# Layer 3's block mix as diagonal matmuls on TensorE, with the gathers of layers 2 and 3 cut and reordered by quarters

## The chip, the cores and the metric

The program runs on one core of a Trainium2 chip. A core has TensorE (PE: matmuls; its weight loads are shown as PEld), VectorE (DVE), ScalarE (ACT), GpSimd (POOL) and SyncE (SP), each with its own instruction queue, which they execute in order; they wait for each other by semaphores. Transfers go through 16 DMA engines. The metric is the device time of one execution in microseconds (us); lower is better.

## The reference

Input: x of 4 sequences of 1,024 tokens of width 128, float32. Four layers, each an attention-like block and a feed-forward block, with a residual and a layer norm after each:

```
x = layernorm(x + L2_attn(x))     # 16 causal heads of width 8
x = layernorm(x + L2_ffn(x))      # 8 experts, the best 2 of each token
x = layernorm(x + L3_attn(x))
x = layernorm(x + L3_ffn(x))      # 32 experts, the best 4, and a shared expert
```

(the last two of the four layers). The change is about L3_attn, and about the rows that the experts of L2_ffn and L3_ffn hand back. L3_attn takes the first axis, the 4 sequences, as the one that it mixes over; every position stands for itself:

```
rms = |q| / sqrt(128);  x = q / (rms + 1e-8)
u = silu(x @ u_w + u_b);  v = silu(x @ v_w + v_b)      # 256 features each
y[i] = sum over j of coefficient(head, i - j) * v[j]    # i, j = 0..3: the sequences
out = (u * y) @ o_w + o_b + q
```

The sum over j is a Toeplitz product over the 4 sequences: seven coefficients, for the lags -3 to 3, for each of 8 heads of 32 features. So in a layout with features on the partitions, a coefficient is a number for each partition.

## The kernel before, in words

x stays in SBUF as 32 tiles of 128 tokens x 128. Eight tiles are a quarter (the same 256 positions of all 4 sequences). Layer 3's parts are a (quarters 0 and 1, "the first half"), b (the third quarter) and c (the fourth). Layer 2's experts have parts too: a2 is the first half, m2 sequences 0 and 1 of the second half, n2 sequences 2 and 3 of it.

**Experts.** A route computes for each token the experts, the weights and the positions in a list ordered by expert (`posl2n`, `posl3a` and so on are these positions; DVE does nearly all of it, with `positions`, L1231). `spread` (L1307) writes the rows of x to the list in HBM by indirect DMAs of POOL, one for each tile and choice (`l3ra<-x`). The experts read the list in order, 512 rows at a time (`gathered`, L1322, `xg<-l3ra`): PE transposes (`tp`), multiplies by gate and up weights (`gu`), ACT takes silu (`sg`), DVE the product (`hg`), PE transposes it and multiplies by the down weights (`yp`), and the rows go back to HBM (`l3ya<-yg`). `collect` (L1350) gathers a token's rows by indirect DMAs of POOL into a tile `yt` and adds them to x with their weights on DVE (L1361). With 8 tiles of `yt`, the ninth gather waits for the adds of the first tile. Layer 3's parts have 64 (a), 32 (b) and 32 (c) indirect DMAs each way; m2 and n2 have 16 each way.

**Attention of layer 3** (`l3_attn`, L1512). For each quarter: norm (L185: statistics L191 and L192, the root, then one DVE `tensor_scalar` for each of 8 tiles, L205), the rms of each token by a square (L1548), a sum (L1549) and a root, the scaled copy `sq`, and x replaced by 2x + o_b (L1564). PE transposes `sq`, multiplies by the weights of v and u; silu on ACT (L1531), for part a by a tanh on ACT and two DVE operations (L1535, L1536), since other exponentials run beside it (`exps`). Then, for each of two groups of 128 features, four output sequences i and four input sequences j, a DVE operation on 128x256: the first a product (L1590), the others multiply-adds (L1592), and a product with u (L1594 or L1596). PE multiplies by o_w (`py`), DVE adds it to x (L1605), and a second norm and transposes follow.

**Order.** A planner written as Python generators writes out each engine's order. `mix` (L233) takes a step of a main generator and then as many steps of a side generator as its declared costs (the numbers that are yielded) fill; `chain` puts generators one after the other, `abreast` interleaves by declared cost, `press` (L1800) runs the side alone until something is done. In each queue the side's instructions keep the place that they got. The stretch that matters, from L1824 `all`:

- main `l2_attn(1)`, the second half's attention of layer 2; side: part a's rows of layer 2 gathered and added, `l3_attn(a)`, `l3_route(a)` and its scatter, with the routes of m2 and n2 in between;
- main `l2_experts(m2)`, with the same side, then `press` until n2's list is written and the route of a done;
- main `l2_experts(n2)`; side: the scatter of a, the gathers of m2 (`rows_in`);
- main shared expert and experts of layer 3 for a; side: the gathers of n2, attention and route of b, then the scatter of b and the gathers of all of a (`last(a)`: `collect`, `finish`), abreast with attention and route of c, then the scatter of c and the gathers of b;
- main shared expert and experts for b, then for c, with the same side; and at the end `close(c)`, the gathers of c with the last norm.

Of the kernel before, what the change touches and what calls it, by code (L numbers as in the profile page):

```python
# [14 lines left out]
AF = mybir.ActivationFunctionType  # L15
# [5 lines left out]
P = 128  # L21
# [48 lines left out]
def tile_of(b, i):  # L70

    return i // 2 * QT + b * 2 + i % 2


class Kernel:
# [109 lines left out]
    def norm(self, tiles, by="act"):  # L185
# [11 lines left out]
        else:  # L197
            ve = self.tile(self.small, [P, n], f"ve{n}")
            nc.vector.tensor_scalar(ve, mv[:, :, 1], LN_EPS, None, ALU.add)
            if by == "pool":  # L200
                nc.gpsimd.tensor_tensor(rstd, ve, self.mhalf[:, :n], ALU.pow)
            else:
                self.rsqrt(rstd, ve)
        for t, x in enumerate(tiles):
            nc.vector.tensor_scalar(x, x, mv[:, t, 0:1], rstd[:, t : t + 1], ALU.subtract, ALU.mult)  # L205
# [1144 lines left out]
    def collect(self, lay, part, k, yp, first=0, nt=None):  # L1350
# [15 lines left out]
        for t in range(first, first + (nt or part.nt)):  # L1366
# [145 lines left out]
    def l3_attn(self, part, exps=False):  # L1512
# [5 lines left out]
        with ExitStack() as ctx:  # L1518
# [19 lines left out]
            for q in range(part.q0, part.q0 + part.nq):  # L1538
                s = slice(q * QT, (q + 1) * QT)
                self.norm(self.quarter(q), by="dve" if exps else "act")  # L1540
                yield (7.0,)
                xq = self.tile(vp, [P, QC], "xq")
                rms = self.tile(self.small, [P, QT], "rms")
                for g in range(2):
                    sg = slice(q * QT + g * 4, q * QT + g * 4 + 4)
                    r = rms[:, g * 4 : g * 4 + 4]
                    sq = self.tile(vp, [P, 4, D], "sq")
                    nc.vector.tensor_tensor(sq, x[:, sg, :], x[:, sg, :], ALU.mult)  # L1548
                    nc.vector.tensor_reduce(r, sq, AX.X, ALU.add)  # L1549
# [524 lines left out]
```

## Time and profile before

| what | value |
|---|---|
| time, median of 15 runs | 2529.88 us (2516.64 to 2544.39) |
| the profiled execution's own time | 2531.99 us |
| its span in the profile | 2530.1 us, granted clock 0.825 |
| busy: PE, DVE, ACT, POOL | 67%, 53%, 33%, 30% |
| layer 2's second attention | 1262 to 1680 us |
| experts of m2, then n2 | 1680 to 1795, 1795 to about 1950 |
| shared expert and experts of layer 3, part a | 1951 to 2114 |
| the same for b, for c | to about 2350, to 2476 |
| the gathers of c and the end | 2476 to 2530 |

The profile names an instruction by its line in the kernel, its engine and operation, and the tiles that it writes and reads (`y<-v,ld,y`). A helper's line stands for all that the helper does: L157 is every matmul, L165 every transpose, L1295 every indirect DMA. "Idle before" is the time that the engine stood before such an instruction, and what released it. In the chain of waits, "issue" and "another core or an unknown queue" are times for which the profile shows no work that was waited for; on one core, the second can only be a handoff whose sender had been done earlier.

### The profile page before, as it was taken

How to read it: one execution, taken by the hardware profiler on the slowest of the kernel's cores; microseconds unless marked ns; L12 is line 12 of the kernel's file. 1: busy time of each engine (PE TensorE's matmuls, PEld its weight loads, DVE VectorE, ACT ScalarE, POOL GpSimd, SP SyncE). 2: the span in 40 equal slices, each digit the busy share in tenths (PEclk: the TensorE clock that was granted, in tenths of full speed). 3: DMA queues.
4: the chain of work that ended last, by engine and by line, in shares of the span. 5: the costliest groups of instructions: out<-in, count | busy, mean ns of one | idle time of the engine just before them, and what ended most of it. 6: DMA issues, size and time to landing. Idle time of an engine off the chain costs nothing.

```text
span 2530.1 us, 28678 instructions
## 1 busy us (share of the span) xinstructions
PE 1704.3 (67%) x9605; PEld 1033.4 (41%) x9605; DVE 1344.9 (53%) x3801; ACT 829.2 (33%) x1193; POOL 769.8 (30%) x701
## 2 busy tenths in 40 slices
PE   7535775985652864877878788978718896373490
PEld 3224333852320433755523232345415684162280
DVE  8857894655550643334536674654603575263363
ACT  5510461432320431322246454622202353131140
POOL 5521384136045004213231002001470204536404
PEclk9756788997775977998889898988869998587795
DMA  9900002434100032312210000030410231132242
GB/s 306 288 2 0 16 34 87 120 129 160 47 30 38 27 125 91 106 47 59 84 54 16 1 1 18 1 128 32 167 64 23 81 115 65 39 108 76 67 126 60
DMA packets 225736, 192.05 MB, mean 76 GB/s; under 512 B 17009, under 2 KB 204273, under 8 KB 225073
## 3 DMA queue, kind: packets, MB, share of 16 engines
q1 hardware_dynamic: 204880, 147.28, 18.4%
q0 software_dynamic: 20704, 42.86, 5.4%
q8 instruction: 83, 1.36, 0.2%
q14 instruction: 69, 0.56, 0.1%
HBM read 93.47 MB, written 96.60 MB: 75 GB/s over the span
## 4 chain that ended last, share of the span: by engine, by line
PE 37%; another core or an unknown queue 16%; DVE 15%; issue 7%; DMA 3%; ACT 3%; POOL 2%; SPq 0%; DVEq 0%; POOLq 0%; ACTq 0%
PE gu L157 10%; PE s L157 9%; PE sc L157 5%; PE yp L157 5%; PE tp L165 4%; POOL yt L1295 2%; DVE x L205 1%; DVE pr L1057 1%; ACT pr L1051 1%; PE py L157 1%; DVE x L1361 1%; DVE bn L191 1%; PE pu L157 1%; PE s L165 1%
## 5 line engine op out<-in xcount | busy, mean ns | idle before, releaser
L1051 ACT ACTIVATE pr<-sc 128x1024 f32<-128x1024 f32 x288 | 279.7, 1021 | 330.3 <-PE sc L157 206.6
L157 PE MATMUL gu<-ld,xgT 128*128 x768 | 203.4, 409 | 97.0 <-ACT xgT L167 46.8
L157 PE MATMUL sc<-qm,kT 32*128 32x512 f32 (+3 forms) x1536 | 200.7, 563 | 15.9 <-issue 14.4
L157 PE MATMUL s<-pr,va 128*32 128x512 f32 (+3 forms) x1536 | 179.4, 536 | 45.2 <-issue 27.2
L157 PEld LDWEIGHTS gu<-ld,xgT 128*128 128x128 f32 x768 | 146.2, 202 | 128.1 <-ACT xgT L167 66.6
L157 PE MATMUL gu<-wall,xgT 128*128 x352 | 178.9, 634 | 2.7 <-ACT xgT L167 2.0
L169 DVE COPY hT<-tp 128x512 f32<-128x512 f32 x140 | 95.9, 685 | 146.0 <-remote 77.3
L165 PE MATMUL tp<-ld,hg 128*128 128x128 f32 x736 | 117.7, 282 | 80.4 <-DVE hT L169 42.0
L1693 DVE TENSOR_TENSOR hg<-sg,gu 128x256 f32<-128x256 f32 x192 | 78.7, 416 | 137.0 <-ACT sg L1692 129.2
L165 PEld LDWEIGHTS tp<-ld,hg 128*128 128x128 f32 x736 | 93.9, 146 | 139.0 <-issue 66.9
L1057 DVE TENSOR_TENSOR pr<-pr,ld 128x512 f32<-128x512 f32 (+1 forms) x160 | 92.5, 581 | 106.4 <-ACT pr L1051 103.9
L167 ACT COPY xgT<-tp 128x512 f32<-128x512 f32 x118 | 69.1, 586 | 216.0 <-PE tp L165 147.2
L1692 ACT ACTIVATE sg<-gu 128x256 f32<-128x256 f32 x192 | 72.7, 384 | 195.4 <-PE gu L157 97.9
L157 PEld LDWEIGHTS sc<-qm,kT 32*128 32x128 f32 x1536 | 85.4, 199 | 122.0 <-issue 80.2
L1466 ACT ACTIVATE sg<-gu 128x512 f32<-128x512 f32 x88 | 52.4, 598 | 235.5 <-PE gu L157 143.2
L1295 POOL DMA_INDIRECT l1ra<-x,posl1a x64 | 94.6, 1478 | 61.2 <-DVE posl1a L1272 42.0
L165 PE MATMUL tp<-ld,xg 128*128 128x128 f32 x472 | 77.9, 290 | 47.9 <-issue 13.9
L157 PE MATMUL yp<-ld,hT 128*128 x768 | 103.6, 278 | 4.2 <-issue 2.5
L1295 POOL DMA_INDIRECT yt<-l1yr,posl1r x64 | 60.8, 949 | 148.6 <-DVE x L1361 73.8
L157 PEld LDWEIGHTS s<-pr,va 128*32 128x32 f32 x1536 | 38.8, 113 | 156.0 <-issue 109.9
L1468 DVE TENSOR_TENSOR hg<-sg,gu 128x512 f32<-128x512 f32 x88 | 60.0, 682 | 77.1 <-ACT sg L1466 69.0
L157 PE MATMUL yp<-wall,hT 128*128 x704 | 98.3, 285 | 1.5 <-DVE hT L169 1.5
(433 smaller groups left out, 3548.8 us busy)
## 6 DMA issues: line engine op xcount, KB each, us to landing
wall<-wall SPq DMA_DIRECT2D x16, 768.0 KB
l3ra<-zero SPq DMA_DIRECT2D x1, 6144.0 KB
ld<-in_l_w SPq DMA_DIRECT2D x2, 3072.0 KB
wall<-we SPq DMA_DIRECT2D x24, 256.0 KB
ld<-in_l_w SPq DMA_DIRECT2D x1, 6144.0 KB
xg<-l3ra SPq DMA_DIRECT2D x24, 256.0 KB
l3ya<-yg SPq DMA_DIRECT2D x24, 256.0 KB
l1ra<-zero SPq DMA_DIRECT2D x1, 5120.0 KB
```

Of the source, the lines that this page charges most:

```text
L157: return self.nc.tensor.matmul(out, lhsT, rhs, start=start, stop=stop)
L165: nc.tensor.transpose(pt[:, k * P : (k + 1) * P], s, self.ident)
L167: nc.scalar.copy(dst, pt[:, : n * P])
L169: nc.vector.tensor_copy(dst, pt[:, : n * P])
L191: nc.vector.bn_stats(st, x)
L1051: nc.scalar.activation(pr, sc[h], AF.Exp)
L1057: nc.vector.tensor_tensor(d, d, cst["tril"].unsqueeze(1).unsqueeze(1).to_broadcast([P, 2, n, P]), ALU.mult)
L1295: ins = self.nc.gpsimd.indirect_dma_start(**kw)
L1466: nc.scalar.activation(sg, gu[:, 0, :], AF.Silu)
L1468: nc.vector.tensor_tensor(h, sg, gu[:, 1, :], ALU.mult)
L1692: nc.scalar.activation(sg, pg[:, :, 0, :], AF.Silu)
L1693: nc.vector.tensor_tensor(h[:, 2 * c : 2 * c + 2, :], sg, pg[:, :, 1, :], ALU.mult)
```

## The change

1. For the attention of parts b and c, the mix moves from DVE to PE. `l3_mixes` builds 14 matrices of 128x128 with a coefficient on the diagonal (7 lags, 2 groups of features), one DVE operation each, on the side between the scatter of a and the gathers of m2. A matmul with such a matrix adds a coefficient times a block of v into PSUM; five matmuls make two output blocks, and one DVE product with u reads them from PSUM. Part a keeps the mix on DVE.
2. In the same two parts, norm is applied by ACT (`Identity` with a scale and a bias, which takes one small DVE operation) instead of DVE's L205.
3. In all parts the rms comes from the norm's variance and root, once for a quarter, so square and sum go; the bias o_b is added by a matmul of a row of ones, and x = 2x + py is one DVE operation.
4. The gathers of n2 are in two pieces: tiles 0, 1, 4, 5 (the third quarter) first, then attention and route of b abreast with tiles 2, 3, 6, 7. They use the 8 tiles of `l3y`.
5. The gathers of part a are in two quarters: the first abreast with attention and route of c as before, the second behind the scatter of c and ahead of the gathers of b. `finish` works on one quarter.

POOL's order of indirect DMAs was: scatter a 64, gathers m2 16, gathers n2 16, scatter b 32, gathers a 64, scatter c 32, gathers b 32, gathers c 32. It becomes: the same up to scatter b, then gathers a 32, scatter c 32, gathers a 32, gathers b 32, gathers c 32. The counts stay. On DVE, the route of a, which stood behind the last product of m2's experts, now lies between their products.

The diff (the path that is only taken if a check of the values fails is left out):

```diff
@@ -182,7 +182,8 @@
             ts(t, t, -0.5, 1.5, ALU.mult, ALU.add)
             tt(y, y, t, ALU.mult)
 
-    def norm(self, tiles, by="act"):
+    def norm(self, tiles, by="act", on_act=False):
+
 
         nc, n = self.nc, len(tiles)
         mv = self.tile(self.small, [P, n, 2], f"mv{n}")
@@ -201,8 +202,15 @@
                 nc.gpsimd.tensor_tensor(rstd, ve, self.mhalf[:, :n], ALU.pow)
             else:
                 self.rsqrt(rstd, ve)
+        if on_act:
+            off = self.tile(self.small, [P, n], f"off{n}")
+            nc.vector.scalar_tensor_tensor(off, mv[:, :, 0], -1.0, rstd, ALU.mult, ALU.mult)
         for t, x in enumerate(tiles):
-            nc.vector.tensor_scalar(x, x, mv[:, t, 0:1], rstd[:, t : t + 1], ALU.subtract, ALU.mult)
+            if on_act:
+                nc.scalar.activation(x, x, AF.Identity, bias=off[:, t : t + 1], scale=rstd[:, t : t + 1])
+            else:
+                nc.vector.tensor_scalar(x, x, mv[:, t, 0:1], rstd[:, t : t + 1], ALU.subtract, ALU.mult)
+        return mv, rstd
 
     def quarter(self, q):
 
@@ -1347,7 +1355,7 @@
                 out=rows.rearrange("(t p) d -> p t d", p=P), in_=self.zero.unsqueeze(1).to_broadcast([P, tl, D])
             )
 
-    def collect(self, lay, part, k, yp, first=0, nt=None):
+    def collect(self, lay, part, k, yp, first=0, nt=None, which=None):
 
         nc = self.nc
         pos, wk, _, _ = self.route[lay + part.name]
@@ -1363,7 +1371,7 @@
                     ALU.mult, ALU.add,
                 )
 
-        for t in range(first, first + (nt or part.nt)):
+        for t in which or range(first, first + (nt or part.nt)):
             yt = self.tile(yp, [P, k, D], "yt")
             for i in range(k):
                 self.indirect(
@@ -1536,35 +1544,28 @@
                 stt(dst, pz, col["l3_b"][:, i : i + 1], dst, ALU.add, ALU.add)
 
             for q in range(part.q0, part.q0 + part.nq):
-                s = slice(q * QT, (q + 1) * QT)
-                self.norm(self.quarter(q), by="dve" if exps else "act")
+                mv, rstd = self.norm(self.quarter(q), by="dve" if exps else "act", on_act=not exps)
                 yield (7.0,)
                 xq = self.tile(vp, [P, QC], "xq")
+
                 rms = self.tile(self.small, [P, QT], "rms")
+                if exps:
+
+                    v = self.tile(self.small, [P, QT], "rmsv")
+                    nc.vector.tensor_scalar(v, mv[:, :, 1], 1e-30, None, ALU.max)
+                    self.rsqrt(rms, v)
+                    nc.vector.tensor_tensor(rms, rms, mv[:, :, 1], ALU.mult)
+                else:
+                    nc.scalar.activation(rms, mv[:, :, 1], AF.Sqrt)
+                nc.vector.tensor_tensor(rms, rms, rstd, ALU.mult)
+                nc.vector.tensor_scalar(rms, rms, 1e-8, None, ALU.add)
+                nc.vector.reciprocal(rms, rms)
+                yield (2.0,)
                 for g in range(2):
                     sg = slice(q * QT + g * 4, q * QT + g * 4 + 4)
+                    sq = self.tile(vp, [P, 4, D], "sq")
                     r = rms[:, g * 4 : g * 4 + 4]
-                    sq = self.tile(vp, [P, 4, D], "sq")
-                    nc.vector.tensor_tensor(sq, x[:, sg, :], x[:, sg, :], ALU.mult)
-                    nc.vector.tensor_reduce(r, sq, AX.X, ALU.add)
-                    if exps:
-
-                        ri = self.tile(self.small, [P, 4], "rmsi")
-                        v = self.tile(self.small, [P, 4], "rmsv")
-                        nc.vector.tensor_scalar(v, r, 1e-30, None, ALU.max)
-                        self.rsqrt(ri, v)
-                        nc.vector.tensor_tensor(r, r, ri, ALU.mult)
-                    else:
-                        nc.scalar.activation(r, r, AF.Sqrt)
-                    nc.vector.tensor_scalar(r, r, float(np.float32(D ** -0.5)), 1e-8, ALU.mult, ALU.add)
-                    nc.vector.reciprocal(r, r)
-                    yield (4.0,)
                     nc.vector.tensor_tensor(sq, x[:, sg, :], r.unsqueeze(2).to_broadcast([P, 4, D]), ALU.mult)
-
-                    stt(
-                        x[:, sg, :], x[:, sg, :], 2.0, self.row["l3_ob"].unsqueeze(1).to_broadcast([P, 4, D]),
-                        ALU.mult, ALU.add,
-                    )
                     yield (2.3,)
                     self.transposes(
                         ps, xq[:, g * BLK : (g + 1) * BLK], [sq[:, k, :] for k in range(4)], on_act=not exps, tag="s"
@@ -1579,10 +1580,24 @@
                             self.mm(pz, wuv[:, i, c * P : (c + 1) * P], xq[:, g * BLK : (g + 1) * BLK])
                             silu(dst[:, 2 * g : 2 * g + 2, :].rearrange("p b t -> p (b t)"), pz, i * NC + c)
                             yield (2.3,)
+                    if not exps:
+
+                        for i0 in range(0, B, 2):
+                            y = self.tile(ps, [P, 2, TQ], "s")
+                            lags = [0, -1, -2, -3, 1] if i0 == 0 else [0, 1, 2, 3, -1]
+                            for lag in lags:
+                                lo, hi = max(i0, lag), min(i0 + 2, B + lag)
+                                self.mm(
+                                    y[:, lo - i0 : hi - i0, :], self.mixes[:, c * 7 + (lag if lag >= 0 else 3 - lag), :],
+                                    v[:, lo - lag : hi - lag, :], lag == 0, lag == lags[-1],
+                                )
+                            nc.vector.tensor_tensor(u[:, c, i0 : i0 + 2, :], u[:, c, i0 : i0 + 2, :], y, ALU.mult)
+                            yield (4.5,)
+                        continue
 
                     cf = col["toep"][:, c * 7 : (c + 1) * 7]
                     for i in range(B):
-                        y = self.tile(vp, [P, TQ], "y", bufs=1 if exps else 2)
+                        y = self.tile(vp, [P, TQ], "y", bufs=1)
                         for j in range(B):
                             lag = i - j
                             a = lag if lag >= 0 else 3 - lag
@@ -1590,26 +1605,33 @@
                                 nc.vector.tensor_scalar(y, v[:, j, :], cf[:, a : a + 1], None, ALU.mult)
                             else:
                                 stt(y, v[:, j, :], cf[:, a : a + 1], y, ALU.mult, ALU.add)
-                        if exps:
-                            stt(u[:, c, i, :], u[:, c, i, :], 0.25, y, ALU.mult, ALU.mult)
-                        else:
-                            nc.vector.tensor_tensor(u[:, c, i, :], u[:, c, i, :], y, ALU.mult)
+                        stt(u[:, c, i, :], u[:, c, i, :], 0.25, y, ALU.mult, ALU.mult)
                         yield (3.0,)
                 for g in range(2):
                     py = self.tile(ps, [P, 4, D], "s")
                     for k in range(4):
                         b, h = (g * 4 + k) // 2, k % 2
+                        self.mm(py[:, k, :], self.cst["all1"][0:1, :], self.row["l3_ob"][0:1, :], True, False)
                         for c in range(NC):
-                            self.mm(py[:, k, :], u[:, c, b, h * P : (h + 1) * P], wo[:, c, :], c == 0, c == NC - 1)
+                            self.mm(py[:, k, :], u[:, c, b, h * P : (h + 1) * P], wo[:, c, :], False, c == NC - 1)
                     sg = slice(q * QT + g * 4, q * QT + g * 4 + 4)
-                    nc.vector.tensor_tensor(x[:, sg, :], py, x[:, sg, :], ALU.add)
+                    stt(x[:, sg, :], x[:, sg, :], 2.0, py, ALU.mult, ALU.add)
                     yield (3.0,)
-                self.norm(self.quarter(q), by="dve" if exps else "act")
+                self.norm(self.quarter(q), by="dve" if exps else "act", on_act=not exps)
                 yield (6.0,)
                 for g in range(2):
                     self.turned(ps, q * QT + g * 4, on_act=not exps, tag="s")
                     yield (2.3,)
 
+
+    def l3_mixes(self, ctx):
+
+        mp = self.pool(ctx, "l3m", right=True)
+        self.mixes = self.tile(mp, [P, 14, P], "mixes")
+        for k in range(14):
+            self.nc.vector.tensor_scalar(self.mixes[:, k, :], self.ident, self.col["toep"][:, k : k + 1], None, ALU.mult)
+            if k % 4 == 3:
+                yield (1.0,)
 
     def l3_route(self, part):
         nc = self.nc
@@ -1735,18 +1757,17 @@
     def l3_experts(self, part, wall):
         return self.small_experts("l3", E3, part, wall)
 
-    def finish(self, part):
-
-        for q in range(part.q0, part.q0 + part.nq):
-            self.norm(self.quarter(q))
-            yield (5.0,)
-            for b in range(B):
-                t = tile_of(b, 2 * q)
-                self.nc.sync.dma_start(
-                    out=self.out[b, q * TQ : (q + 1) * TQ, :].rearrange("(k p) d -> p k d", p=P),
-                    in_=self.x[:, t : t + 2, :],
-                )
-            yield (1.0,)
+    def finish(self, q):
+
+        self.norm(self.quarter(q))
+        yield (5.0,)
+        for b in range(B):
+            t = tile_of(b, 2 * q)
+            self.nc.sync.dma_start(
+                out=self.out[b, q * TQ : (q + 1) * TQ, :].rearrange("(k p) d -> p k d", p=P),
+                in_=self.x[:, t : t + 2, :],
+            )
+        yield (1.0,)
 
     def chain(self, *gens):
         for g in gens:
@@ -1806,9 +1827,10 @@
         yield from self.l2_route(part)
         yield from self.spread("l2", part, K2)
 
-    def last(self, part, yp):
-        yield from self.collect("l3", part, K3, yp)
-        yield from self.finish(part)
+    def last(self, part, yp, q=0):
+
+        yield from self.collect("l3", part, K3, yp, q * QT, QT)
+        yield from self.finish(part.q0 + q)
 
     def close(self, part, yp):
 
@@ -1870,17 +1892,22 @@
                     self.run(self.mix(self.l2_experts(m2, wall), on, drain=False))
                     self.press(on, lambda: {"l2n", "routed l3a"} <= self.listed)
                     sw, wall3 = self.l3_wall(c3, True)
-                    on = self.chain(on, self.rows_in(m2))
+                    on = self.chain(on, self.l3_mixes(c3), self.rows_in(m2))
                     self.run(self.mix(self.l2_experts(n2, wall), on, drain=False))
                 self.press(on, listed("l3a"))
                 yp = self.pool(c3, "l3y", 8)
+
                 on = self.chain(
-                    on, self.rows_in(n2), self.l3_attn(b), self.l3_route(b),
+                    on, self.collect("l2", n2, K2, yp, which=(0, 1, 4, 5)),
                     self.abreast(
-                        self.chain(self.spread("l3", b, K3), self.when(listed("made l3a")), self.last(a, yp)),
+                        self.chain(self.l3_attn(b), self.l3_route(b)),
+                        self.collect("l2", n2, K2, yp, which=(2, 3, 6, 7)),
+                    ),
+                    self.abreast(
+                        self.chain(self.spread("l3", b, K3), self.when(listed("made l3a")), self.last(a, yp, 0)),
                         self.chain(self.l3_attn(c), self.l3_route(c)),
                     ),
-                    self.spread("l3", c, K3), self.when(listed("made l3b")), self.last(b, yp),
+                    self.spread("l3", c, K3), self.last(a, yp, 1), self.when(listed("made l3b")), self.last(b, yp),
                 )
                 self.run(self.mix(self.chain(self.l3_shared(a, sw), self.l3_experts(a, wall3)), on, 0.75, False))
                 self.press(on, listed("l3b"))
...
```

More of the change, by code (lines that the diff above doesn't have):

```diff
@@ L1902, in all @@
                     self.run(self.rows_in(p))
+                self.run(self.l3_mixes(ctx))
                 for p in self.parts:
@@ L1907, in all @@
                         self.run(self.l3_shared(p, sw), self.l3_experts(p, wall))
-                        self.run(self.last(p, self.pool(c2, "l3y" + p.name, 5)))
+                        yp = self.pool(c2, "l3y" + p.name, 5)
+                        self.run(*(self.last(p, yp, q) for q in range(p.nq)))
 @with_exitstack
```

## The prediction

> **What bounds the kernel now.** I read the page's engine totals first, then the shares of the chain that ended last, then a table of stretches from the second attention of layer 2 to the end, then the waits of POOL, then the chain inside the stretches where POOL works, then the costs of the operations that the change names.
>
> ```profile
> PE 1704.3 (67%) x9605; PEld 1033.4 (41%) x9605; DVE 1344.9 (53%) x3801; ACT 829.2 (33%) x1193; POOL 769.8 (30%) x701
> ...
> PE 37%; another core or an unknown queue 16%; DVE 15%; issue 7%; DMA 3%; ACT 3%; POOL 2%; SPq 0%; DVEq 0%; POOLq 0%; ACTq 0%
> ```
>
> No engine is full. PE leads the chain, but 23% of it is idle time with no visible cause (the second and fourth entries). The table of stretches (window, length, busy PE, PEld, DVE, ACT, POOL, clock, DMA share, GB/s) says where that is:
>
> ```profile
> 1262.00:1680.00 418.00, 340.78 (x2402) 130.03 (x2402) 238.02 (x727) 213.95 (x227) 47.19 (x48) 0.89 0.09 33
> 1772.00:1795.00 23.00, 14.56 (x75) 9.82 (x74) 21.43 (x103) 5.18 (x8) 0.00 (x0) 0.90 0.19 58
> 1795.00:1903.00 108.00, 43.84 (x175) 26.84 (x173) 18.88 (x29) 11.53 (x20) 77.32 (x80) 0.71 0.34 126
> 1996.00:2114.00 118.00, 109.84 (x673) 92.98 (x673) 89.12 (x287) 62.27 (x114) 0.16 (x1) 0.97 0.37 111
> 2114.00:2196.00 82.00, 25.43 (x67) 12.07 (x66) 20.37 (x50) 13.15 (x18) 62.05 (x64) 0.61 0.18 56
> 2236.00:2292.00 56.00, 41.31 (x240) 36.18 (x239) 36.90 (x142) 18.46 (x37) 30.14 (x32) 0.88 0.41 116
> 2351.00:2396.00 45.00, 13.02 (x49) 7.06 (x47) 10.15 (x48) 4.85 (x8) 30.33 (x32) 0.68 0.27 70
> ```
>
> Two kinds of stretch: where POOL issues indirect DMAs without a break (1795, 2114, 2351), PE, DVE and ACT nearly stop together; where it doesn't (1996), PE is full. At 2236 POOL issues in batches of eight and PE keeps 41 of 56 us. The row at 1772 is a third kind: DVE is full with the router of part a, and PE works off the end of the second-layer experts. The waits of POOL and the chain agree:
>
> ```profile
> POOL l3rb L1295 <- DVE posl3b L1272: 120.1, 1, 120.1
> ...
> POOL l3ra L1295 <- DVE posl3a L1272: 71.3, 1, 71.3
> ...
> 2133.75 14.76 issue
> 2148.55 1.28 ACT L735
> 2149.84 8.56 another core or an unknown queue
> 2158.44 9.76 another core or an unknown queue
> ...
> 2361.21 35.31 another core or an unknown queue
> ```
>
> POOL starts each scatter when the positions are ready, and from then on handoffs between engines come 5 to 35 us late. So the end is about the POOL runs plus the PE work between them. Check from 2114 to the end, 416 us: 192 indirect issues at 1.26 us (0.96 busy and 0.30 issue) are 242; 160 us of PE work at full clock (198 busy, a good part of it at 0.5 to 0.7) and 14 us after the last gather make 416.
>
> Durations of the operations (groups, mean ns):
>
> ```profile
> L1592 DVE SCALAR_TENSOR_TENSOR y<-v,ld,y 128x256 f32<-128x256 f32 x96 | 43.7, 480 | 6.9 <-issue 5.4
> L205 DVE TENSOR_SCALAR x<-x,mv,rstd 128x128 f32<-128x128 f32 x112 | 31.2, 348 | 0.6 <-DVE rstd L196 0.2
> L1590 DVE TENSOR_SCALAR y<-v,ld 128x256 f32<-128x256 f32 x32 | 10.8, 353 | 22.5 <-ACT v L1531 22.4
> L1651 DVE TENSOR_TENSOR x<-py,x 128x512 f32<-128x512 f32 x8 | 5.5, 692 | 74.1 <-remote 55.2 <-PE py L157 18.9
> L157 PE MATMUL gu<-ld,xgT 128*128 x448 | 119.1, 411 | 58.0 <-ACT xgT L167 46.5 <-DVE hg L1693 9.9 <-DVE mv L192 1.2
> ```
>
> **The change part by part.** The sum is against the profiled execution, 2531.99 us with a span of 2530.1; it lies 2.1 us above the median of 2529.88.
>
> *DVE work taken out.* Per quarter of parts b and c: mix 8 x 0.353 + 24 x 0.480 + 8 x 0.421 (the multiply by u) = 17.7 us; two squares and two sums at 0.68 = 2.7; two scalings of x at 0.69 = 1.4; 16 norm applications at 0.348 = 5.6, which go to ACT. Added: four multiplies from PSUM at 0.69 (the row of the add of py, also from PSUM) = 2.8 and two small ones at 0.17. Net 24 us less DVE each. Each quarter of part a keeps the DVE mix and saves 2.7 + 1.4 + 2.6 (a second Newton chain, some 16 small operations at 0.165) = 6.7. ACT: the 16 applications lie between its rows of 301 ns (128x8) and 384 ns (128x256), 5 us a quarter; ACT is busy 62 of 118 us there, so I cost them at nothing. If that cover went, it would be the 5 us.
>
> *PE work put in.* A mix of a quarter is 20 matmuls over 8,192 columns; at 411 ns for 256 columns that is 13.2 us, at the 512-column rows (0.68 to 0.78) nearer 12. The bias is 8 matmuls at 0.275 = 2.2 per quarter, in all four. So +4.4 us for part a, +15 for b, +15 for c.
>
> *Layer 2's second attention, 1262 to 1680.* PE 341 of 418 busy, and its waits there name DVE for some 40 us. DVE loses 13, PE gains 4.4. But the last norm of part a now stands on PE's order before the second-layer experts (its 8 statistics, small operations and 8 applications are 9 us; they lay inside the experts). Bounds -10 and +8; I take -3, since waits on DVE outweigh added PE work.
>
> *Route of part a.* In the instruction order its DVE work now lies among the experts' tiles instead of after them. The experts' last gate product was at 1778 and the positions were ready at 1795: at most 17 us go, plus what the earlier start of the experts gives. DVE is busy 42 of 92 us from 1680 to 1772, so there is room for the 21 us; bounds -24 and -4 (every tile stretched by a DVE turn). I take -18. POOL's scatter and all behind it come that much earlier. If that wait goes, what is late next is the same 64-issue run.
>
> *The 14 diagonals.* 14 x 0.348 = 4.9 us of DVE in experts whose 108 us are held by POOL, where DVE does 19: nothing; 5 if the cover is gone.
>
> *Layer 2's last gathers.* The same 16 issues, the third quarter's 8 first, from 8 buffers. Part b's attention can start 8 x 1.26 = 10 us earlier after them. That attention has the shared expert and the experts of part a beside it, 163 us of which PE is busy 152: worth 0, bounds -10 and +3 (the second 8 still sit ahead of part b's scatter on POOL).
>
> *Experts of part a, 1996 to 2114.* PE is the bound: +15. Against it: PE's idle 8 us of 118, and the DVE end of the route of b (2104 to 2114), of which the masking moves ahead: -5. Bounds: +15 and -10 (all DVE waits gone); I take +2, for 8 and 5 against 15.
>
> *After 2114.* POOL's count of issues stays 192. Before, the order was scatter b, 64 gathers of part a (32 unbroken, 32 in batches), scatter c, gathers b, gathers c; now the second 32 of part a come behind scatter c, as one unbroken run, and the gathers of b, queued behind them on POOL, wait for buffers that the adds inside the experts of c free, so they come in batches. One unbroken run of 32 is exchanged for another: nothing. Part c's attention has 15 more PE and 24 less DVE; four new handoffs from PE to DVE stand where handoffs come 5 to 15 us late. The adds of b, 32 x 0.345 = 11 us, move beside the last gathers, where DVE is busy 17 of 54: nothing, or 11 if they come ahead of the last adds. Bounds -25 and +35; I take +3.
>
> Sum: -3 - 18 + 0 + 0 + 2 + 3 = -16. The profile would read 2516, the median 2514.
>
> **Two rules beside the rows.** From 2114 to 2196 PE is busy 25 of 82 us, at a clock of 0.61, while POOL issues. The Trainium skill, page "SBUF — State Buffer", section "Who interferes with whom", says that only VectorE and GpSimd share ports and that "PE and ACT never wait on anyone". By that rule a POOL run should leave PE alone, the tail would go by PE's own work, and its term would be +15 and not +3; this trace differs from it, and I go by the trace. For the clock of 0.61 there is the page "TensorE: Matmul & The Clock Gate", section "What's actually happening": an idle window of about 3.4 us halves the clock. It speaks against this change: matmuls moved into POOL runs would take twice their time, 24 us for the mix of c instead of 12, and the sum would be -4.
>
> **Rivals.** *Slower: the mix of part c falls into the POOL run.* Its products start beside scatter b, where handoffs took 4.9 to 14.8 us; four at 9 are 36 us, with 15 of PE and less some 10 of DVE: +41 in place of +3, so 2514 + 38 = 2552. For it: attention c's activations ended at 2185 and 2197, inside and just behind the run. Against: most of attention c follows at 2196 to 2280, beside experts. It decides once the two middle handoffs cost more than 16 us together. *More gained.* The gathers of b in batches cost what the row at 2236 shows, 15 of 56, instead of the 35 us of the freeze at 2361, and the new gathers behind scatter c find PE stopped anyway: -20 more, 2494. Against: the unbroken run grows from 32 to 64. *Nothing moves.* The experts' tiles stretch by what the route of a puts between them, each tile needing three DVE turns, and 15 us of PE come on top in experts a: 2528.
>
> **How the numbers follow.** Forecast 0.36 (2500 to 2524), more gained 0.22, nothing moves 0.15, the mix in the run 0.27. This kernel's runs tell about 0.3% (7.6 us) from no change. Faster: 0.31 of the forecast, 0.22, and 0.04 of the third: 0.57. Same: 0.04 + 0.06 + 0.01 = 0.11. Slower: the rest, 0.32. The range reaches from the second rival less 16 (2478) to the first plus 4 (2556).
>
> **What would show it.** Right: posl3a ready at about 1775 with its run following; DVE of L1592 only for part a; the stretch of shared expert and experts of a at 160 to 170 us; scatter b starting at about 2095; gathers of b in batches inside experts c. Wrong: experts a longer than 180 us, chain pieces from PE to the multiply of u above 5 us after scatter b, or more than 425 us from scatter b to the end.

## The result and the profile after

The changed kernel takes 2593.56 us (median of 9 runs, 2576.40 to 2600.05) beside 2530.87 for the kernel before: a ratio of 1.0244, 95% interval 1.0222 to 1.0265. By the ratio it is some 62 us slower, where 16 us less were forecast. The span of the profiled execution is 2589.3 us.

One thing has to be said ahead of all further numbers. The runs fell on chips of two kinds. The experiments ran on five chips. On two of them, as in the runs and profiles of before and after above, the kernel before takes some 2514 to 2531 us, and handoffs between engines come late while POOL issues. On the other three it takes 2102 to 2105 us, and PE, ACT and DVE work on beside POOL. Each of the five ran at one time only, so whether the kind belongs to the chip or to the time is not shown. Kernels are compared by their ratios to before on the same chip; the two kinds are called the late chips and the prompt chips below.

The engine totals of the page after, then the shares of its chain:

```profile
PE 1757.7 (68%) x9749; PEld 1070.1 (41%) x9749; DVE 1298.0 (50%) x3655; ACT 828.8 (32%) x1213; POOL 771.4 (30%) x701
...
PE 37%; another core or an unknown queue 14%; DVE 13%; issue 6%; DMA 3%; ACT 3%; POOL 1%; SPq 0%; DVEq 0%; POOLq 0%; ACTq 0%
```

DVE has lost 47 us of work and PE has gained 53. By the forecast's own terms PE should have gained 34 (4.4 + 15 + 15).

Stretches of the kernel after (window, length, busy PE, PEld, DVE, ACT, POOL, clock, DMA share, GB/s):

```profile
2020.00:2144.00 124.00, 119.42 (x704) 97.85 (x704) 67.02 (x215) 59.68 (x119) 0.00 (x0) 1.00 0.31 92
2144.00:2185.00 41.00, 24.96 (x58) 10.44 (x56) 9.89 (x37) 12.11 (x22) 31.06 (x32) 0.83 0.16 60
2185.00:2225.00 40.00, 2.08 (x2) 0.50 (x2) 0.69 (x1) 0.00 (x0) 30.32 (x32) 0.52 0.20 53
2309.00:2390.00 81.00, 18.76 (x80) 15.64 (x79) 14.16 (x54) 7.26 (x12) 61.44 (x64) 0.61 0.26 80
2455.00:2533.00 78.00, 52.29 (x317) 46.62 (x315) 42.96 (x127) 24.27 (x49) 30.56 (x32) 0.86 0.41 117
```

In the first row, the experts of a, PE is full (119 of 124) and DVE half idle: the DVE work that went bought nothing. The third row is the run of gathers behind scatter b: PE does 2 us in 40. The fourth is the new unbroken run of scatter c and the second 32 gathers of a. The last is the experts of c, which now have the gathers of b beside them.

A table by stage shows where the 62 us arise. It counts from the moment that the positions of layer 2's first half are ready (949 to 964 us in these traces; before it the kernels do the same). All columns are profiled executions on the two late chips of the experiments. The column "rms, norm on ACT" is the kernel before with the rms from the variance and norm on ACT; each column to the right adds one part. A product is DVE's multiplication of `hg`.

| us after that moment | before | rms, norm on ACT | + n2's gathers in two | + gathers of a in quarters | + mix on PE | after (+ bias by one row) |
|---|---|---|---|---|---|---|
| positions of n2 | 735 | 719 | 720 | 729 | 722 | 742 |
| positions of a | 826 | 801 | 801 | 811 | 804 | 822 |
| last product of n2's experts | 979 | 970 | 969 | 981 | 971 | 991 |
| positions of b | 1148 | 1137 | 1138 | 1151 | 1161 | 1181 |
| fourth product of b's experts | 1255 | 1248 | 1258 | 1271 | 1285 | 1312 |
| positions of c | 1318 | 1307 | 1316 | 1310 | 1318 | 1345 |
| last product of c's experts | 1499 | 1498 | 1514 | 1527 | 1533 | 1559 |
| end | 1562 | 1561 | 1576 | 1593 | 1598 | 1625 |
| **time against before** | 1 | 1.0043 | 1.0079 | 1.0112 | 1.0148 | 1.0244 |

Traces of kernels that are alike up to a point differ there by up to 13 us (1138 and 1151 for the positions of b), so single steps of the table are rough; its last row is timed.

### The profile page after: what moved, and what is told of

Same layout as the page of the kernel before. It is cut to its first block, busy times and chain, and to the rows that moved or that the text cites. A ratio compares the mean times of both kernels' runs of the same rounds, so it can differ in the third digit from the quotient of the medians.

```text
span 2589.3 us, 28834 instructions
## 1 busy us (share of the span) xinstructions
PE 1757.7 (68%) x9749; PEld 1070.1 (41%) x9749; DVE 1298.0 (50%) x3655; ACT 828.8 (32%) x1213; POOL 771.4 (30%) x701
## 4 chain that ended last, share of the span: by engine, by line
PE 37%; another core or an unknown queue 14%; DVE 13%; issue 6%; DMA 3%; ACT 3%; POOL 1%; SPq 0%; DVEq 0%; POOLq 0%; ACTq 0%
PE gu L157 10%; PE s L157 9%; PE sc L157 5%; PE yp L157 4%; PE tp L165 4%; PE py L157 1%; PE pg L157 1%; PE pu L157 1%; ACT pr L1059 1%; DVE pr L1065 1%; DVE x L1369 1%; POOL yt L1303 1%; DMA xg<-l2rn 1%; DVE bn L192 1%
## 5 line engine op out<-in xcount | busy, mean ns | idle before, releaser
L157 PE MATMUL s<-pr,va 128*32 128x512 f32 (+3 forms) x1536 | 171.8, 528 | 48.4 <-issue 25.9
```

What stands on the lines that cost most here:

```text
L157: return self.nc.tensor.matmul(out, lhsT, rhs, start=start, stop=stop)
```

## The experiments

The first four undo one part of the changed kernel each; the others put parts back to how they were, until little is left. Three suspicions were named: theory 1, the diagonal mix of c is caught by late handoffs; theory 2, the new order of the gathers costs; theory 3, PE is the bound and added matmuls come out as time.

### One part undone (prompt chip)

**Part c, or b and c, with the mix on DVE:**

```diff
-                    if not exps:
+                    if part.name not in ('a', 'c'):            # the other: ('a', 'b', 'c')
                         for i0 in range(0, B, 2):
```

> The changed kernel (2593 us, 1.024 of before), but part c mixes on DVE as before; part b stays on TensorE. Theory 1 (handoffs of the diagonal mix stuck in POOL's run after scatter b, two of 23 us in the trace of the changed kernel): the stretch from scatter b to the first expert group of b shrinks by about 18 us, time near 2570, ratio 1.015. Theory 2 (the new order of the gathers is what costs): no change beyond 5 us. Theory 3 (added matmuls of 15 us a part): about 10 less, from PE time alone, spread over the experts of b.

> Parts b and c both mix on DVE; norm on ACT, rms from the variance, the bias by matmul and the new order of the gathers stay. Theory 3: a further 12 to 15 us less than with c alone on DVE, in the stretch of shared expert and experts of a (154 us in the changed kernel from the end of n2's gathers to scatter b, 121 before). Theory 1: nearly the same time as with c alone on DVE. Theory 2: both within 5 us of the changed kernel.

**All 64 gathers of a ahead of scatter c:**

```diff
-    self.chain(self.spread("l3", b, K3), self.when(...), self.last(a, yp, 0)),
+    self.chain(self.spread("l3", b, K3), self.when(...), self.last(a, yp, 0), self.last(a, yp, 1)),
...
-    self.spread("l3", c, K3), self.last(a, yp, 1), self.when(...), self.last(b, yp),
+    self.spread("l3", c, K3), self.when(...), self.last(b, yp),
```

> The changed kernel, but all 64 gathers of part a stand ahead of scatter c again. Theory 2: the 24 us that the experts of c lose to the gathers of b (in batches) go, and the experts of b lose about 15 to gathers of a in batches; the run after scatter c is 41 us long and not 81, the gathers of b freeze 35: net 10 to 30 less, 2565 to 2583. Theories 1 and 3: same within 5 us, since the number of indirect DMAs is the same and only the place moves.

**n2's gathers in one piece:**

```diff
-    on, self.collect("l2", n2, K2, yp, which=(0, 1, 4, 5)),
-    self.abreast(self.chain(self.l3_attn(b), self.l3_route(b)), self.collect(..., which=(2, 3, 6, 7))),
+    on, self.rows_in(n2), self.l3_attn(b), self.l3_route(b),
```

> The changed kernel, but the 16 gathers of n2 in one piece ahead of part b's attention, in their old buffers. If the 16 in one run cost the shared expert of a its time (the run 1961 to 1980 with PE's handoffs late), 5 to 10 us less. Otherwise the same within 3 us.

Measured, against 2105.49 for before: c on DVE 1.0123 (1.0103 to 1.0143), b and c on DVE 1.0046 (1.0025 to 1.0067), gathers whole 1.0202 (1.0181 to 1.0223), n2's in one piece 1.0137 (1.0118 to 1.0156). The changed kernel itself later had one run on another prompt chip, with 2121.3 us beside 2102.52, about 1.009. So there the mix of b costs 15 us (2131.05 less 2115.70; theory 3: the positions of b stood 14 us earlier without it). The other three can only be set against that single run, by the ratios: undoing the mix of c alone gains nothing, undoing the quarters makes it some 24 us slower, undoing n2's two pieces some 10. Both new orders of the gathers gain, then, and theory 2 is wrong on this kind of chip.

### The whole, before, and two ladders (late chips)

> The changed kernel itself beside the kernel before, since the first four runs fell on a chip on which before takes 2105 us and not 2530 and nothing stops beside POOL's runs. If the chip of these runs is of that kind: undoing any one part gave ratios of 1.005 to 1.020 there, so the whole change should lie at 1.013 to 1.022, with scatter b starting at the same time as with c alone on DVE (the mix of c comes later) and the rest to the end 283 us or a little more. If it is of the other kind: 1.024 as recorded.

> The kernel before, for its trace on this chip: where it is not stopped beside POOL's runs, scatter b should start about 152 - 15 = 137 us after the last gather of n2, and from there to the end take about 282 us, as POOL's 192 issues of 1.26 us (242) and 40 more.

Measured: 1.0241 (1.0211 to 1.0272); this chip was a late one, and the result is confirmed. The trace of before is the column in the table.

**Nothing added to PE; and the kernel before with only rms, norm on ACT and the bias by matmul:**

```diff
+    stt(x[:, sg, :], x[:, sg, :], 2.0, <l3_ob on 4 tiles>, ALU.mult, ALU.add)
...
-    self.mm(py[:, k, :], self.cst["all1"][0:1, :], self.row["l3_ob"][0:1, :], True, False)
...
-    stt(x[:, sg, :], x[:, sg, :], 2.0, py, ALU.mult, ALU.add)
+    nc.vector.tensor_tensor(x[:, sg, :], py, x[:, sg, :], ALU.add)
```

> The changed kernel with everything that it adds to PE taken out: mix of b and c on DVE, the bias added on DVE (eight more DVE operations of 0.69 us in all); norm on ACT, rms from the variance and the order of the gathers stay. If added PE work is what costs (2.2 us of bias a quarter and 12 to 15 of mix for b and c), this is 9 us below the version with both mixes on DVE, at or below the time before: ratio 0.996 to 1.001. If the order of the gathers or norm on ACT costs, it stays at 1.004 or above.

> The kernel before with norm on ACT in b and c, rms from the variance and the bias by matmul; mix and order of the gathers as before. If the order of the gathers helps on such a chip (whole gathers of a: 16 us longer tail; n2's gathers in one piece: scatter b 7 us later), this is slower than the same with the new order (1.0046): about 1.010. If the order costs, below 1.000.

Measured: 1.0112 (1.0085 to 1.0138) and 1.0139 (1.0107 to 1.0170). So neither the order nor added PE work explains it alone. The second was the surprise: no mix, no new order, and 35 us slower. The positions of n2 stood at 742 on the table's count in its trace, as in the kernel after. The same version without the bias matmuls (measured last on a late chip, below) has 719 there, and the two differ in nothing but the way the bias is added; ahead of that point these are 16 matmuls of part a.

**The bias in three ways.** PE's rows for the product with o_w (start, length, engine, line, tiles, shape, count), first in the kernel before, one group of four tiles, then in the kernel after, the same place (both from the traces of the two runs that head this section; weight loads left out):

```profile
1647.89 2.63 PE L157 MATMUL s<-ld,u 128*128 128x128 f32 x16
```

```profile
1655.37 0.48 PE L157 MATMUL s<-rows,ld 1*128 1x128 f32 x2
1655.79 0.79 PE L157 MATMUL s<-ld,u 128*128 128x128 f32 x4
1656.51 0.79 PE L157 MATMUL s<-rows,ld 1*128 1x128 f32 x2
1657.23 1.22 PE L157 MATMUL s<-ld,u 128*128 128x128 f32 x4
1658.38 0.79 PE L157 MATMUL s<-rows,ld 1*128 1x128 f32 x2
1659.11 1.22 PE L157 MATMUL s<-ld,u 128*128 128x128 f32 x4
1660.26 0.79 PE L157 MATMUL s<-rows,ld 1*128 1x128 f32 x2
1660.98 1.22 PE L157 MATMUL s<-ld,u 128*128 128x128 f32 x4
```

From 2.6 us the group has gone to 6.8: two one-row instructions (one float32 matmul) take 0.72 from start to start, and the four behind them 1.15 where they took 0.66. Part of that is the granted clock, which was 0.54 over the group after (1655 to 1672) and 0.67 around the group before (1646 to 1651). The experiment kept the number of matmuls and changed their height: the identity of 128 rows, times the bias that stands on every partition.

```diff
-    self.mm(py[:, k, :], self.cst["all1"][0:1, :], self.row["l3_ob"][0:1, :], True, False)
+    self.mm(py[:, k, :], self.ident, self.row["l3_ob"], True, False)
```

> The changed kernel, with the bias still added by 8 matmuls a group on PE, but of full height: identity (128 rows) times the row that stands on all partitions, in place of a matmul with one row. Theory A (the one-row matmuls break PE's pipelining: 6.6 us for a group of 24 instructions in the trace where 16 without them took 2.6, so 8 us a quarter and 32 in all): about 25 us less than the changed kernel on a chip where before takes 2520, ratio 1.013 to 1.015. Theory B (what counts is the number of matmuls on PE): same as the changed kernel within 4 us.

The other has the bias on DVE, as in the diff above, and the mix on PE.

> The changed kernel with the bias added on DVE as before, the mix of b and c on PE. Theory A: within 6 us of the version with full-height bias matmuls, ratio 1.011 to 1.014. Theory B: 9 us of PE less than the changed kernel, ratio 1.020. Against the version that has also the mixes on DVE (1.011 on such a chip) it tells what the mixes cost: theory 1 says 15 to 20 us more, all behind scatter b.

Measured: 1.0173 (1.0132 to 1.0215) and 1.0148 (1.0099 to 1.0197). The same place in the trace with full height, one pair of each of the two groups:

```profile
1636.66 0.64 PE L157 MATMUL s<-rows,ld 128*128 128x128 f32 x2
1637.09 1.06 PE L157 MATMUL s<-ld,u 128*128 128x128 f32 x4
1637.94 0.64 PE L157 MATMUL s<-rows,ld 128*128 128x128 f32 x2
...
1641.91 0.39 PE L157 MATMUL s<-rows,ld 128*128 128x128 f32 x2
1642.13 0.61 PE L157 MATMUL s<-ld,u 128*128 128x128 f32 x4
1642.58 0.39 PE L157 MATMUL s<-rows,ld 128*128 128x128 f32 x2
```

The clock changes within these rows, so like has to be set beside like. Three stretches (window, length, busy PE, PEld, DVE, ACT, POOL, clock, DMA share, GB/s): the kernel after at this place, the kernel after in part b's quarter, and full height at this place:

```profile
1655.00:1672.00 17.00, 16.89 (x60) 13.10 (x61) 3.06 (x9) 0.00 (x0) 0.00 (x0) 0.54 0.01 1
2094.00:2103.00 9.00, 9.00 (x54) 7.02 (x53) 1.65 (x3) 0.00 (x0) 0.00 (x0) 1.00 0.20 58
```

```profile
1636.00:1645.00 9.00, 8.31 (x58) 7.84 (x57) 2.55 (x7) 0.00 (x0) 0.00 (x0) 0.81 0.00 0
```

At the low clock (0.50 from 1656.3 to 1673.0 with one row, 0.51 from 1636.4 to 1639.8 with full height) a pair takes 0.72 with one row and 0.43 with full height, and the four behind it 1.15 and 0.85. At full clock (the second row above, and 1639.9 to 1644.4) it is 0.41 and 0.22, and 0.64 and 0.45. Besides, the low clock lasts longer with one row: 16.7 us in which PE was busy all the time, against 3.4 with full height. In the other quarters one row ran at full clock throughout; why it doesn't here, no run shows.

In the quarters where the groups run at full clock, both groups together take 3.7 us without the bias, 5.5 with full height, 8.5 with one row; in part a's second quarter, where the clock is low for a part of them or for all, 6.0, 8.2 and 15.2. The positions of n2 stand at 742 with one row and 722 with full height, and these two kernels, on two late chips, differ in the form alone. So theory A holds in its sign, though 25 us were expected: some 18 of the 62 us (1.0244 less 1.0173; 6 to 30 by the intervals) are the form of the bias matmul, some 6, within the intervals, its number. The Trainium skill, page "TensorEngine Tiling (Array Packing)", section "Key Properties", says that changing the tiling mode drains TensorE. Alternating a 1-row and a 128-row matmul would fit that if it is such a change, which the page doesn't say; 0.41 us against 0.22 at full clock is the number beside it. Whether it is a drain, no run here shows.

**What is left without added matmuls:**

> Mix and bias on DVE, norm on ACT, rms from the variance, n2's gathers in two pieces, all 64 gathers of part a ahead of scatter c again. Theory 2: the experts of c, which took 81 us from their first to their last product with gathers of b beside them and 52 before, go back to 52 to 55; the experts of b take back 15 to 25: net 0 to 15 less than with gathers in quarters, ratio 1.005 to 1.011 on a chip with late handoffs; on a chip without them 15 us more.

> The kernel before with only norm on ACT in b and c and rms from the variance: no added matmul, old order of all gathers. The version with the bias on PE besides was at 1.0139. Theory A: 25 us less, 1.002 to 1.004. If 1.000 or below, the smaller DVE work gains; if it stays above 1.008, norm on ACT costs by itself.

The diffs are those of the whole gathers, and in the second also n2's gathers in one piece, on top of the version with nothing added to PE. Measured: 1.0079 (1.0052 to 1.0106) and 1.0043 (1.0020 to 1.0067). From 1.0043 by 1.0079 to 1.0112, n2's pieces cost about 9 us and the quarters about 8 on a late chip; neighbouring intervals touch, the ends don't. In the traces the experts of c take 81 us from their fourth to their last product with the quarters and 52 without, as theory 2 said; what lies before them gives 15 back.

### Rms alone, with and without the quarters (prompt chips)

From the version at 1.0043, the norm of b and c goes back to DVE; the second also has the gathers of a in quarters, as in the changed kernel.

```diff
-    self.norm(self.quarter(q), by="dve" if exps else "act", on_act=not exps)
+    self.norm(self.quarter(q), by="dve" if exps else "act")
```

> The kernel before with the rms from the variance alone: norm on DVE, bias on DVE, mix on DVE, old order of all gathers. The version with norm on ACT besides measured 1.0043, although its scatter b started 11 us earlier in the trace: the gain was gone behind scatter b, where ACT and PE waited for late handoffs. If norm on ACT (two more handoffs between DVE and ACT for each quarter) costs it, this is at 0.995 to 1.000 and beats both kernels. If not, 1.003 to 1.005.

> The same with the gathers of part a in two quarters, the second behind scatter c. Theory 2: the gathers of b, which then wait for buffers inside the experts of c, cost 8 to 16 us against the version with rms only. If the order is only moved (counts alike), the same within 4 us.

> The changed kernel once more beside these: on a chip where before takes some 2520 us, 2585 (1.024); on one where it takes 2105, 2145 to 2160, since the version with whole gathers and everything else was at 1.020 there.

> The version with rms from the variance alone, for a chip where before takes some 2520 us and handoffs come late beside POOL's runs. There: 0.997 to 1.004 if norm on ACT was what cost in the version at 1.0043; 1.004 or above if the smaller DVE work itself doesn't pay behind scatter b. On a chip where before takes 2105: 1.007 as measured.

> The same with the gathers of part a in two quarters. On the chip with late handoffs 8 to 16 us above the version without (as between the two versions with norm on ACT), so 1.002 to 1.010, and the sign of this part depends on the chip; on the other 0.997 as measured.

> The kernel before, for its trace beside these two. On the chip without late handoffs scatter c, gathers b and gathers c should not run on without a break as they do with the quarters: 20 to 30 us of POOL waiting between them.

All of these ran on prompt chips, the changed kernel with the 2121.3 us told above instead of 2145 to 2160. Measured: rms alone 1.0073 (1.0047 to 1.0099) and again 1.0079 (1.0048 to 1.0109); with the quarters 0.9966 (0.9949 to 0.9984) and again 0.9959 (0.9941 to 0.9976). So the same part has opposite signs: 20 to 23 us gained here, about 8 lost on a late chip. The waits of POOL from scatter b to the end say why it gains; first the kernel before, then rms with the quarters (engine, tile, line, who ended the wait: total, times, longest):

```profile
POOL yt L1295 <- DMA l3yc<-yg: 32.6, 1, 32.6
```

```profile
POOL l3rc L1303 <- DVE mv L193: 12.9, 1, 12.9
...
POOL yt L1303 <- DMA l3yc<-yg: 0.3, 1, 0.3
```

On a prompt chip POOL is the bound of the end. With scatter c ahead of the second gathers of a, the experts of c are done before POOL gets to their rows, and the wait of 32.6 us is gone for one of 12.9. On a late chip the gathers of c start 8 us after the experts' last product, without the quarters and with them, and the gathers of b beside the experts of c cost these 29 us (81 against 52). Rms with the quarters is 0.3 to 0.4% faster than before on a prompt chip, and faster than the changed kernel's single run there; on a late one it wasn't run, and what norm on ACT costs there, and so why the version at 1.0043 isn't faster than before, stays open.

**Why rms alone loses 16 us**, though it only takes work away: the queue of SP. First the kernel before, then rms alone, same chip (start, length, engine, line, transfer, count):

```profile
1559.16 15.78 SPq L1326 DMA_DIRECT2D xg<-l2rn  x4
1575.03 0.46 SPq L153 DMA_DIRECT2D ld<-in_l_sw  x1
1577.80 0.35 SPq L153 DMA_DIRECT2D ld<-in_l_w  x1
```

```profile
1559.10 0.36 SPq L1334 DMA_DIRECT2D xg<-l2rn  x1
1559.56 0.49 SPq L153 DMA_DIRECT2D ld<-in_l_sw  x1
1561.26 0.35 SPq L153 DMA_DIRECT2D ld<-in_l_w  x1
1561.66 37.34 SPq L1334 DMA_DIRECT2D xg<-l2rn  x4
```

Before, all four loads of n2's list that were ready went ahead of layer 3's weights (one of these transfers is 6 MB); now one does, and the others stand behind them. PE pays, in the waits of rms alone and of the kernel after on a late chip:

```profile
PE tp L165 <- DMA xg<-l2rn: 15.5, 2, 10.2
```

```profile
PE tp L165 <- DMA xg<-l2rn: 15.1, 2, 9.9
```

The kernel before has no such wait. On the prompt chips the positions of a are ready 17 us earlier with rms alone (683 us against 700 on the table's count) and n2's experts end 12 later (784 against 772). On a late chip POOL's run for the scatter of a releases n2's experts 22 us earlier in the version at 1.0043 (first product behind it at 920 against 942), but 17 products are then left where 13 were before, and the gain at their end is 9; PE waits 15.0 us for the list there too. That the loads' place is the cause is read from the traces; a version with the weights moved behind the loads wasn't run.

## Why the prediction was wrong, point by point

The forecast summed to -16, and +62 was measured. By the table (after less before) the difference arises in three places: up to the last product of n2's experts +12 where -21 was forecast, from there to the positions of b +22 where +2 was, and behind them +29 where +3 was.

**The bias: a term mis-sized, and the largest.** "8 matmuls at 0.275 = 2.2 per quarter" took a row of 128-row matmuls for one-row ones. Full height would have kept the price: 5.5 less 3.7 is 1.8. One row cost 4.8 at full clock and 9.2 in the quarter in which the clock stayed low: 23 us for four quarters in the traces, where 8.8 were forecast, and 24 by the times (1.0139 less 1.0043). A mean duration of a pipelined matmul says nothing of what a change of shape does to its neighbours.

**Layer 2's second attention, -3.** PE begins with the list of m2's experts at 709 before, at 703 without the bias, at 726 with it: 6 us earlier, within the bounds, then 17 later. The term's mechanism was right, its sign was turned by the bias.

**Route of part a, -18.** The positions came 25 us earlier without the bias (801 against 826), 6 of them from the attention, so the hiding worked, as said. But "all behind it come that much earlier" failed: n2's experts ended only 9 earlier. What was late next was named as POOL's run; it was the list load behind the weights on SP, of which the forecast said nothing, though SP's order of work moved too. The page before also had the other half: in the row at 1772, PE did 14.6 of 23 us, so as far as PE is the bound only 8 could be gained there.

**Experts of part a, +2.** From n2's last product to the positions of b: 168 us before, 170 with the quarters and no matmul added, 190 with the mix. These 20 are more than the mix's own time, 14.4 us in the trace of the kernel after (four groups of 3.6, where 12 to 13.2 were forecast); on a prompt chip the same step was 14. PE was full in its row, and the 13 us set against the added 15 were not there: what PE waited for was not what DVE lost.

**Norm on ACT, nothing.** An application took 482 ns on ACT, where 301 to 384 were the bounds; no run here prices it alone.

**N2's gathers, 0, and behind scatter b, +3.** From the positions of b to the end: 414 before, 424 with rms and norm on ACT, 438 with n2's pieces, 442 with the quarters, 437 with the mix, 443 after. Here it was +29. "One unbroken run of 32 is exchanged for another: nothing" missed that batches beside experts cost 29 us there, and that a late chip gives back only part. That is the smaller share of the +29: the steps of 10 with rms and norm on ACT and of 14 with n2's pieces are larger, and no run here gives their cause.

**The rivals.** None of their times came near the result; the slowest said 2552. The one on the other side had the sign. Its mechanism is to be seen after scatter b, where the last of the first products of the mix ended at 2182 (rows of PE, then of DVE, in the kernel after):

```profile
2175.37 6.74 PE L157 MATMUL s<-v,mixes 128*128 128x512 f32 x18
```

```profile
2205.41 0.69 DVE L1594 TENSOR_TENSOR u<-u,s 128x512 f32<-128x512 f32 x1 [45.40 <-issue]
2230.96 0.69 DVE L1594 TENSOR_TENSOR u<-u,s 128x512 f32<-128x512 f32 x1 [24.86 <-remote]
```

Two handoffs of 23 and 25 us, against 9 that were priced, and far above the 16 together from which the rival was to decide. Yet taking the mix away left the end as it was (442 against 437): other handoffs were late in its place, with pieces of 21.8 and 21.1 us in the chain behind scatter b of the version with nothing added to PE. So a late handoff that can be seen in a trace isn't a price; that the run of POOL is, whoever waits in it, fits this but was not tested. "More gained" by the batches of b fell on late chips, and came true in another way on prompt ones.

**The rules beside the rows.** The prediction read the rule on shared ports as saying that a POOL run leaves PE alone. That holds on the prompt chips (PE 99 of 105 us busy from 1595 to 1700 in the version with c on DVE, beside 78 indirect DMAs) and not on the late ones; what differs was not found, and whether ports have a part in it isn't shown. The clock rule's fear, twice the time, came true by a small part where it was meant: of c's mix, one half took 8.6 us at a granted clock of 0.83 in the first trace of the kernel after and 10.1 at 0.70 in the second, against 7.1 to 7.2 for the other half at full clock. It came true more fully in a place that wasn't meant: the bias matmuls of part a's second quarter ran at 0.54, with PE busy 16.9 of 17 us, against 0.81 over the same work at full height.

## What to carry to other kernels

A matmul's price is its time from start to start among its neighbours, so look for a change of shape before taking a row's mean; here a bias of one row was cheaper as an identity of full height, and no dearer on the engine where it was. When a wait is hidden, follow every queue past it, SP's too: here large weight loads slipped ahead of small ones, for which PE then waited 15 us. Where a stage's engine is full, as PE in the experts of a, work moved onto it is paid in full and work taken from another buys nothing.

## What the hardware showed unexpectedly

The same kernel takes 2102 to 2105 us on three chips and 2514 to 2521 on two others, and what the engines do beside POOL's indirect DMAs differs between them; a reordering of these gained 1% on the one kind and cost some 0.3% on the other. At full clock a one-row matmul between full ones took 0.41 us where one of full height took 0.22, and the four instructions behind it 0.64 where they took 0.45. In one quarter the clock also stayed at 0.50 for 16.7 us with one row, though PE was busy all the time, and for 3.4 us with full height.
